# Mixing single accumulating transfers among the pair transfers of a segment sum, and six instead of twelve of them in front

## The chip, the cores and the metric

The kernel runs on one core of a Trainium2 chip. The metric is device time in microseconds (us), the median of several executions. The core's engines are TensorE (PE; PEld in the profile is its weight load), VectorE (DVE), ScalarE (ACT), GpSimd (POOL) and SyncE (SP, which here only issues transfers).

## What is computed

A layer of a graph network. There are N = 6250 nodes and 206250 edges, each with 128 features in float32; `row` is the source node of each edge.

```python
edge_aggr = jnp.zeros((n, HIDDEN), dtype=x.dtype).at[row].add(edge_features)
reps = n // global_feat.shape[0]
global_expand = jnp.repeat(global_feat, reps, axis=0)
combined = jnp.concatenate([x, edge_aggr, global_expand], axis=-1) @ W_c + b_c
h = jax.nn.softplus(combined @ W1 + b1)
h = jax.nn.softplus(h @ W2 + b2)
return h @ W3 + b3            # then: layernorm(x + this)
```

Nearly all of the time goes into the first line, the segment sum.

## The kernel before

**Two kinds of edges.** The edges are cut into columns, and every column takes one of two ways to the sum.

- *Pairs* (810 pairs of columns, 105 edges in a column). The edges are sorted into buckets of 256 nodes. ACT or DVE writes a one-hot matrix (`compare`, L869 and L876/L878), TensorE multiplies by it (`gather`, L887), ACT copies the result out of PSUM into one of six `pairs` buffers (`settle`, L898), and POOL sends each pair of columns with one indirect transfer to its place in a DRAM table `place` (L932). When a group of pairs is complete, SP reads `place` back as `chunks` (L579, issued through L176), DVE makes one-hots (`match`, L587), TensorE multiplies (`product`, L604), and DVE adds into `sums_t` (L617).
- *Own columns* (283, 128 edges in each). Edges of the same node are merged inside the column: TensorE spreads the node numbers (`name_own`, L810), DVE compares (`equal_own`, L819), TensorE sums (`sum_own`, L829), ACT copies (`ready_own`, L840), DVE writes the row numbers (`number_own`, L847/L849). POOL then adds the column to a copy of the totals in DRAM with one accumulating indirect transfer (L916). There are three copies, taken in turn; the first twelve own columns use copies 0 and 1 only, since copy 2 is zeroed later (`zero(2)`). An addition to a copy waits until the one before it on that copy has landed. The copies are read back and joined at the end.

**Groups and pieces.** There are nine groups, with (own, pairs) of (18, 20), (14, 80), (22, 130), four times (31, 130), (66, 40), (20, 20), and 19 own columns after the last pair. The two `place` tables alternate from group to group. Own columns and pairs are handled in pieces of up to three columns or three pairs. In each group the pieces are merged by their relative position, so that pieces of three own lie evenly among the pieces of three pairs; in group 0, LEAD = 12 own columns stand ahead of the first pair.

**The order of the work.** The order on TensorE, DVE, ACT and SP is the order in which the program emits the steps. It comes from planned times: the first transfer at FIRST = 13 us, then SCATTER = 1.3 us for every pair and ADDED = 1.87 us for every own column. Every piece's earlier steps are placed ahead of its planned time: its rows are loaded 34 us ahead, the gather 14 us, the settling copy 10.5 us, and so on. `over(...)` spreads other work over a span of the plan: the positions for the next group's pairs (`positions`, L343 to L556), the filling of the next table (`fill_rows`), and the reduction of the group before (`reduce_steps`, L558). All events are sorted by planned time and emitted. POOL's transfers are tied to the emitted order wherever an own column is next to another transfer.

The reduction of a group starts at the start of the next group. Its first chunk load on SP waits until all pair transfers of its group have landed, and whatever SP issues after it waits too.

The transfers of POOL share eight completion semaphores in turn. A settling copy reuses a `pairs` buffer six pieces later and waits for the three transfers out of it.

Of the kernel before, what the change touches and what calls it, by code (L numbers as in the profile page):

```python
# [13 lines left out]
ALU = mybir.AluOpType  # L14
# [36 lines left out]
COPIES = EACH  # L51
EARLY = (0, 1) * 6


SCATTER, ADDED = 1.3, 1.87
LOADED, CODED, COMPARED, GATHERED, SETTLED = 34.0, 21.0, 17.5, 14.0, 10.5
NAMED, EQUALLED, SUMMED, READY, NUMBERED = 20.0, 17.5, 14.0, 10.5, 7.5
FIRST = 13.0
LEAD = 12
SHARES = {0: 2, 1: 2, 2: 2}  # L60
SHARE = 3
PREP, SUM, FILLED = 0.85, 0.97, 0.6
# [7 lines left out]
BANKS = 3  # L70

TABLES = 6
NO_SYNC = mybir.DependencyInfo(mybir.DependencyClass.NoSync, mybir.DependencyReason.SCHED_ONLY)


@with_exitstack
def kernel(
# [23 lines left out]
    nc = tc.nc  # L101
# [67 lines left out]
    def copy_rows(k, a, b):  # L169
        return totals_at[k][a:b, :]  # L170
# [4 lines left out]
    def put_dma(engine, out, in_):  # L175
        ins = engine.dma_start(out, in_).ins  # L176
        if put["last"] is not None and put["tied"]:
            tc.add_manual_dep(ins, put["last"].name, NO_SYNC, reason="one order of all transfers")
        put["last"] = ins

    def rows_dma(out, in_):
        for _ in range(2):
# [2 lines left out]
        put_dma(nc.sync, out, in_)  # L185

    def sync_dma(out, in_):
        put_dma(nc.sync, out, in_)

    def node_rows_of(pool, n0, n, bufs=2):  # L190
        t = pool.tile([P, 4, D], F32, name="x_sb", bufs=bufs)
# [7 lines left out]
    with ExitStack() as phase:  # L199
# [358 lines left out]
        def reduce_steps(g):  # L558
# [16 lines left out]
            def load(i):  # L575
                b, lo, hi, _ = loads[i]
                t = chunks_p.tile([P, LOAD_CHUNKS, ROW], F32, name="chunks")
                chunks[i] = t
                sync_dma(t[:, :hi - lo].rearrange("p j c -> p (j c)"),  # L579
                         src_rows[(b * room + lo) * P:(b * room + hi) * P, :].rearrange(  # L580
                             "(p j) c -> p (j c)", p=P))

            def match(n):
                i, a, e = halves[n]
# [63 lines left out]
        def node_rows():  # L648
# [91 lines left out]
            steps.append(lambda: store(blocks_at[-1]))  # L740
            return steps

        pieces, ring, pair_no = [], {}, {}
        LATE = groups[-1][1]

        def own_pieces(g, a, b):
            own = [(g, "own", c, min(EACH, min(b, T) - c), P) for c in range(a, min(b, T), EACH)]
            if R and a < b == TC:
                own.append((g, "own", T, 1, R))
            return own  # L750

        for g, (a, b, _, _, s0, s1) in enumerate(groups):
            own = own_pieces(g, a, b)
            pairs = [(g, "pair", t, min(PAIRS, s1 - t), P) for t in range(s0, s1, PAIRS)]
            lead = 0 if g else LEAD // EACH
            mixed = sorted([((k + 0.5) / len(l), l[0][1], l[k]) for l in (own[lead:], pairs) if l
                            for k in range(len(l))])
            pieces += own[:lead] + [m[2] for m in mixed]
        last_pair = len(pieces) - 1
        pieces += own_pieces(G - 1, LATE, TC)  # L760
        for i, piece in enumerate(pieces):
            if piece[1] == "own":
                ring[i] = len(ring)
# [142 lines left out]
                nc.gpsimd.reg_mov(limits[rows], rows)  # L906
            return limits[rows]

        def scatter_rows(i):
            g, kind, c, k, r = pieces[i]  # L910
            if kind == "own":
                at, rows = own_of.pop(i)
                for j in range(k):
                    n = c + j
                    copy = EARLY[n] if n < len(EARLY) else n % COPIES
                    s = nc.gpsimd.indirect_dma_start(  # L916
                        out=copy_rows(copy, 0, N + 2),
                        out_offset=bass.IndirectOffsetOnAxis(ap=at[:r, j:j + 1], axis=0),
                        in_=rows[:r, j, :D], in_offset=None, bounds_check=limit(N + 1),
                        oob_is_err=False, compute_op=ALU.add)  # L920
                    if issued["last"] is not None:
                        tc.add_manual_dep(s.ins, issued["last"].name, NO_SYNC,
                                          reason="one order of all scatters")
                    issued["last"], issued["own"] = s.ins, True
                return
            rows_at.pop(i)
            rows = sets_at.pop(i)
            dst = places[place_of[g]][:rows_of[g], :].rearrange("(n two) c -> n (two c)", two=2)
            last = rows_of[g] // 2 - 1
            for j in range(k):  # L930
                at = pair_of[g][:, c - groups[g][4] + j:c - groups[g][4] + j + 1]
                s = nc.gpsimd.indirect_dma_start(  # L932
                    out=dst, out_offset=bass.IndirectOffsetOnAxis(ap=at, axis=0),
                    in_=rows[:, j].rearrange("p a b -> p (a b)"), in_offset=None,
                    bounds_check=limit(last), oob_is_err=False)
                if issued["own"]:
                    tc.add_manual_dep(s.ins, issued["last"].name, NO_SYNC,
                                      reason="one order of all scatters")
                issued["last"], issued["own"] = s.ins, False
                tc.declare_no_dep(s.ins, group="scatter",  # L940
                                  reason="no two edges of a group have one position")
                tc.add_to_no_dep_group("scatter", s.ins)

        bucket_at = {}

# [64 lines left out]
        with tc.manual_schedule(engines={ET.PE, ET.DVE, ET.Activation, ET.SP}):  # L1010
# [17 lines left out]
            tables()  # L1028
            nc.vector.memset(fill, -1.0)

            begins = []
            now = FIRST
            for _, kind, _, k, _ in pieces:
                begins.append(now)
                now += (SCATTER if kind == "pair" else ADDED) * k
            early = [i for i, t in enumerate(begins) if t < LOADED]

            def zero(k):
# [31 lines left out]
            def when(t, step):  # L1070
                events.append((t, len(events), step))
# [5 lines left out]
            for i, t in enumerate(begins):  # L1077
                if t >= LOADED:
                    when(t - LOADED, lambda i=i: load_rows(i))
                if pieces[i][1] == "own":  # L1080
                    when(t - NAMED, lambda i=i: name_own(i))
                    when(t - EQUALLED, lambda i=i: equal_own(i))
                    when(t - SUMMED, lambda i=i: sum_own(i))
                    when(t - READY, lambda i=i: ready_own(i))
                    when(t - NUMBERED, lambda i=i: number_own(i))
                else:
                    when(t - CODED, lambda i=i: code_rows(i))
                mine = units(i)
                for u, unit in enumerate(mine):
                    late_by = SCATTER * pieces[i][3] * u / len(mine)  # L1090
                    when(t - COMPARED + late_by, lambda unit=unit: compare(unit))
                    when(t - GATHERED + late_by, lambda unit=unit: gather(unit))
                    when(t - SETTLED + late_by, lambda unit=unit: settle(unit))
                when(t, lambda i=i: scatter_rows(i))
            over([more_tables, lambda: node_codes(0)] + positions(0), -8.0, FIRST + ADDED * LEAD - 19.0)
            over(fill_rows_0, -2.0, FIRST + ADDED * LEAD - 14.0)
            when(FIRST + ADDED * LEAD - 13.0, lambda: zero(2))
            when(4.0, rest_of_nodes)
            for g in range(1, G):
                a, b = groups[g][:2]  # L1100
# [16 lines left out]
            for g in range(G):  # L1117
                mine = [q for q in range(len(pieces)) if pieces[q][0] == g]
                t0 = begins[mine[0]]
                t1 = begins[mine[-1]] + (SCATTER if pieces[mine[-1]][1] == "pair" else  # L1120
                                         ADDED) * pieces[mine[-1]][3]
                prep = []
                for k in range(g + 1 + (g > SOONER), min(G, g + 2 + (g >= SOONER))):
                    prep += [lambda k=k: node_codes(k)] + positions(k)
                if NODES[0] <= g < NODES[1]:
                    upto = len(nodes)
                    if g + 1 < NODES[1]:
                        upto = 3 + (upto - 3) * (g + 1 - NODES[0]) // (NODES[1] - NODES[0]) // 4 * 4
                    part = nodes[held:upto]
                    held = upto  # L1130
                    middle = t0 + PREP * (t1 - t0)
                    over(part, middle, t1)
                    over(prep, t0, middle)
                else:
                    over(prep, max(t0, 34.0), t0 + PREP * (t1 - t0))
                if g == G - 1:
                    middle = max(t0 + 0.65 * (t1 - t0), begins[last_pair] + 9.0)
                    over(reduce_steps(g - 1), t0, middle)
                    over(reduce_steps(g), middle, t1 + 2.0)
                elif g:  # L1140
                    over(reduce_steps(g - 1), t0, t0 + SUM * (t1 - t0))
                over(fill_rows(g + 1), t0, t0 + FILLED * (t1 - t0))
# [284 lines left out]
```

## Time and profile before

| | |
|---|---|
| median of 3 runs | 1998.59 us (1998.35 to 2001.69) |
| profiled execution | 2005.1 us, its span 2002.9 us |
| mean granted clock of TensorE | 0.879 |
| PE busy | 1630.5 us (81%) |
| PEld busy | 1395.4 us (70%) |
| DVE busy | 1233.2 us (62%) |
| ACT busy | 1174.0 us (59%) |
| POOL busy | 1298.9 us (65%) |

Times of a group of instructions are written as busy time, mean of one in ns, idle time of the engine just ahead of them, and what ended most of that idle time. A window's line gives its length and then each engine's busy time in it. In a timeline, the number in brackets is how long the engine was idle before, and what released it; several instructions of one line are drawn together (x6). A busy TensorE can hold waits inside, since the ends of matmuls are modelled.

Group 0's transfers take 24 to 104 us of the span, groups 1 to 6 run from 104 to 1608 us, group 7 to 1788, group 8 to 1853, the 19 late own columns to 1888, and the joining of the copies and the dense layers to the end.

### The profile page before, as it was taken

What the parts mean: (1) busy time and instruction counts of PE and PEld (TensorE: products, weight loads), DVE (VectorE), ACT (ScalarE), POOL (GpSimd) and SP (SyncE); (2) the same over time, 40 slices, a digit from 0 to 9 for tenths busy, and PEclk for the clock granted to TensorE, in tenths of its full rate; (3) what the DMA queues carried; (4) which work ended last, traced back from release to release, by engine and by line L of the source; (5) the groups of instructions that cost most, each with busy time, mean ns of one, the idle gap of its engine ahead of it and who ended that gap; (6) DMA issues with size and microseconds to landing.
All of it is one profiled execution on the core that took longest, in us unless ns stands there. A gap on an engine that the chain in (4) does not pass through costs nothing. (4 is left out here: it accounts for less than half of the span.)

```text
span 2002.9 us, 30974 instructions
## 1 busy us (share of the span) xinstructions
PE 1630.5 (81%) x10093; PEld 1395.4 (70%) x10093; DVE 1233.2 (62%) x2726; ACT 1174.0 (59%) x2921; POOL 1298.9 (65%) x1163
## 2 busy tenths in 40 slices
PE   5567777886889897998898888887888899969585
PEld 4456666775778776887676777766777788868464
DVE  7556645665556664676665776754555467756537
ACT  4255565666766666776677575666776654333045
POOL 2666565666666666666666665557666678778845
PEclk9577677888899989898998898899999899989888
DMA  9686465866777676876767666669777599966872
GB/s 338 164 253 184 140 194 163 236 190 178 214 210 202 196 204 192 237 215 181 209 183 237 190 191 174 185 168 265 207 213 214 156 249 227 229 148 164 211 207 66
DMA packets 401839, 399.72 MB, mean 200 GB/s; under 512 B 34286, under 2 KB 331323, under 8 KB 401673
## 3 DMA queue, kind: packets, MB, share of 16 engines
q1 hardware_dynamic: 322073, 275.77, 47.7%
q0 software_dynamic: 79600, 121.90, 23.5%
q8 instruction: 84, 1.38, 0.3%
q14 instruction: 82, 0.67, 0.1%
HBM read 245.79 MB, written 161.24 MB: 203 GB/s over the span
## 5 line engine op out<-in xcount | busy, mean ns | idle before, releaser
L932 POOL DMA_INDIRECT place<-pairs,pair x810 | 796.3, 983 | 420.9 <-issue 210.1
L604 PE MATMUL part<-hot,chunks 128*128 128x256 f32 x3440 | 928.8, 410 | 68.0 <-DVE hot L587 27.2
L898 ACT COPY pairs<-sorted 64x387 f32<-64x387 f32 (+2 forms) x1100 | 521.4, 474 | 588.3 <-PE sorted L887 213.1
L604 PEld LDWEIGHTS part<-hot,chunks 128*128 128x128 f32 x3440 | 663.2, 206 | 178.5 <-issue 59.7
L587 DVE SCALAR_TENSOR_TENSOR hot<-chunks,both_ps 128x512 f32<-128x512 f32 (+2 forms) x614 | 542.0, 896 | 221.8 <-PE part L604 105.4
L887 PE MATMUL sorted<-rows,sort_hot 105*128 105x129 f32 x3240 | 528.8, 307 | 90.0 <-ACT sort_hot L878 26.6
L887 PEld LDWEIGHTS sorted<-rows,sort_hot 105*128 105x128 f32 x3240 | 483.1, 216 | 156.4 <-issue 45.3
L916 POOL DMA_INDIRECT totals_at<-own_sum,own_at x283 | 440.4, 1556 | 227.7 <-issue 101.2
L876 ACT ACTIVATE sort_hot<-by_slot,slot 105x128 f32<-105x128 f32 x1006 | 331.7, 394 | 3.7
L878 ACT ACTIVATE sort_hot<-sort_hot,ones 105x384 f32<-105x384 f32 (+1 forms) x341 | 208.5, 611 | 11.1
L840 ACT COPY own_sum<-sorted 128x387 f32<-128x387 f32 (+3 forms) x99 | 46.3, 467 | 146.0 <-PE sorted L829 92.9
L869 DVE TENSOR_TENSOR sort_hot<-slot,both_ps 105x384 f32<-105x384 f32 (+1 forms) x209 | 112.5, 539 | 2.7 <-PE sorted L887 2.0
L819 DVE TENSOR_TENSOR same<-sorted,src_i 128x384 f32<-128x384 f32 (+3 forms) x99 | 53.0, 535 | 92.6 <-PE sorted L810 32.5
L423 DVE TENSOR_REDUCE slot<-small 105x20 f32<-105x500 f32 x81 | 54.8, 676 | 87.5 <-remote 29.4
L529 DVE TENSOR_SCALAR pair<-small,half_p 64x10 int32<-64x10 f32 x162 | 36.6, 226 | 114.2 <-remote 53.2
L829 PE MATMUL sorted<-own_rows,same 128*128 128x129 f32 x566 | 94.6, 303 | 9.1 <-issue 7.0
L829 PEld LDWEIGHTS sorted<-own_rows,same 128*128 128x128 f32 x566 | 85.1, 211 | 24.1 <-issue 17.9
L522 PEld LDWEIGHTS <-spread 104*128 104x128 bf16 x810 | 30.9, 100 | 69.7 <-DVE spread L511 39.7
L522 PE MATMUL small<-jump,spread 104*128 104x4 bf16 x810 | 33.7, 166 | 53.7 <-DVE spread L511 31.8
L617 DVE TENSOR_TENSOR sums_t<-sums_t,part 128x512 f32<-128x512 f32 (+1 forms) x104 | 68.3, 660 | 6.8 <-PE part L604 4.9
L417 PEld LDWEIGHTS <-ones_h 104*105 104x105 bf16 x405 | 37.5, 147 | 47.4 <-issue 40.8
L511 DVE TENSOR_TENSOR spread<-both_ps,starts 104x640 bf16<-104x640 f32 x81 | 66.8, 824 | 1.7
(179 smaller groups left out, 1081.6 us busy)
## 6 DMA issues: line engine op xcount, KB each, us to landing
rows<-in_edge_attr SPq DMA_DIRECT2D x266, 315.0 KB
chunks<-place SPq DMA_DIRECT2D x125, 408.0 KB
chunks<-place SPq DMA_DIRECT2D x120, 340.0 KB
own_rows<-in_edge_attr SPq DMA_DIRECT2D x91, 192.0 KB
chunks<-place SPq DMA_DIRECT2D x49, 272.0 KB
place<-pairs,pair POOLq DMA_INDIRECT x810
totals_at<-sums_t SPq DMA_DIRECT2D x3, 3072.0 KB
late<-totals_at SPq DMA_DIRECT2D x36, 256.0 KB
```

Of the source, the lines that this page charges most:

```text
L511: nc.vector.tensor_tensor(past, twice_ps[:KB].unsqueeze(1).to_broadcast([KB, per_set, P]), own["starts"][:, q0:q0 + per_set].unsqueeze(2). ...
L587: nc.vector.scalar_tensor_tensor(hot[:, :e - a], chunks[i][:, a:e, D:W].to_broadcast([P, e - a, BL]), code_of(g), iota_ps.unsqueeze(1).to_ ...
L604: nc.tensor.matmul(part[:, b % 2, :], t[:, q, :D], hot[:, q - a], start=(lo + q == 0), stop=(last and q == hi - lo - 1))
L617: nc.vector.tensor_add(here, here, new)
L829: nc.tensor.matmul(out[:r, j, :], same[:r, j, :r], rows_at[i][:r, j, :], start=True, stop=True)
L869: nc.vector.tensor_tensor(hot[:PN, :m], slot[:PN, at:at + 2 * m - 1:2].unsqueeze(2).to_broadcast([PN, m, P]), slot_ps[:PN].unsqueeze(1).to ...
L876: nc.scalar.activation(hot[:PN, j], by_slot[:PN], AF.Abs, bias=slot[:PN, at:at + 1], scale=-1.0)
L878: nc.scalar.activation(hot[:PN, :m], hot[:PN, :m], AF.Relu, bias=ones[:PN, :1], scale=-1.0)
L887: nc.tensor.matmul(out[:, j, :], hot[:PN, j], rows_at[i][:PN, 2 * (lo + j) + n, :], start=True, stop=True)
L898: nc.scalar.copy(sets_at[i][64 * n:64 * n + 64, lo:lo + m, h, :W], out[64 * h:64 * h + 64, :m, :])
L916: s = nc.gpsimd.indirect_dma_start(out=copy_rows(copy, 0, N + 2), out_offset=bass.IndirectOffsetOnAxis(ap=at[:r, j:j + 1], axis=0), in_=ro ...
L932: s = nc.gpsimd.indirect_dma_start(out=dst, out_offset=bass.IndirectOffsetOnAxis(ap=at, axis=0), in_=rows[:, j].rearrange("p a b -> p (a b ...
```

## The change

Two things change in the order of POOL's transfers.

1. Own columns and pairs of a group are no longer merged by pieces of three but singly: a list `issues` holds (piece, index in the piece), and `scatter_row(i, j)` issues one transfer where `scatter_rows(i)` issued a piece's three. In groups 3 to 6 this puts one own column after every four or five pairs, in groups 1 and 2 after every five or six. A piece's planned time is that of its first transfer.
2. LEAD becomes 6. The end of the spans for `positions(0)` and `fill_rows(0)` hangs on LEAD and moves from 16.4 to 5.2 us and from 21.4 to 10.2 us of the plan; `zero(2)` stays at 22.2 (22.4 before).

Besides, the first chunk load of each group is given explicit dependencies on the last twelve pair transfers of its group.

```diff
-LEAD = 12
+LEAD = 6
+LANES = 12
+SYNC = mybir.DependencyInfo(mybir.DependencyClass.Sync, mybir.DependencyReason.DATA)
...
-                sync_dma(t[:, :hi - lo].rearrange("p j c -> p (j c)"),
+                ins = sync_dma(t[:, :hi - lo].rearrange("p j c -> p (j c)"),
...
+                if i == 0:
+                    for late in lasts[g][-LANES:]:
+                        tc.add_manual_dep(ins, late.name, SYNC, reason="every row is there")
...
             lead = 0 if g else LEAD // EACH
-            mixed = sorted([((k + 0.5) / len(l), l[0][1], l[k]) for l in (own[lead:], pairs) if l
-                            for k in range(len(l))])
-            pieces += own[:lead] + [m[2] for m in mixed]
+            parts = [(p, j) for p in own[lead:] for j in range(p[3])]
+            both = [(p, j) for p in pairs for j in range(p[3])]
+            mixed = [(p, j) for p in own[:lead] for j in range(p[3])] + [
+                m[2] for m in sorted([((k + 0.5) / len(l), l[0][0][1], l[k])
+                                      for l in (parts, both) if l for k in range(len(l))],
+                                     key=lambda m: m[:2])]
+            for p, j in mixed:
+                if not j:
+                    pieces.append(p)
+                issues.append((p, j))
...
-            begins = []
+            begins, ends, at_time = [None] * len(pieces), [None] * len(pieces), []
             now = FIRST
-            for _, kind, _, k, _ in pieces:
-                begins.append(now)
-                now += (SCATTER if kind == "pair" else ADDED) * k
+            for p, j in issues:
+                i = number[p]
+                if not j:
+                    begins[i] = now
+                at_time.append((now, i, j))
+                now += SCATTER if p[1] == "pair" else ADDED
+                ends[i] = now
...
-                when(t, lambda i=i: scatter_rows(i))
+            for t, i, j in at_time:
+                when(t, lambda i=i, j=j: scatter_row(i, j))
             over([more_tables, lambda: node_codes(0)] + positions(0), -8.0, FIRST + ADDED * LEAD - 19.0)
             over(fill_rows_0, -2.0, FIRST + ADDED * LEAD - 14.0)
-            when(FIRST + ADDED * LEAD - 13.0, lambda: zero(2))
+            when(FIRST + ADDED * LEAD - 2.0, lambda: zero(2))
```

`scatter_row(i, j)` holds the same two transfers as `scatter_rows(i)` at L916 and L932, without the loops over `j`, and keeps a list `lasts` of each group's pair transfers.

More of the change, by code (lines that the diff above doesn't have):

```diff
@@ L179, in put_dma @@
         put["last"] = ins
+        return ins
     def rows_dma(out, in_):
@@ L187, in sync_dma @@
     def sync_dma(out, in_):
-        put_dma(nc.sync, out, in_)
+        return put_dma(nc.sync, out, in_)
     def node_rows_of(pool, n0, n, bufs=2):
@@ L741, in node_rows @@
             return steps
+        lasts = {}
         pieces, ring, pair_no = [], {}, {}
         LATE = groups[-1][1]
+        issues = []
         def own_pieces(g, a, b):
@@ L755 @@
             lead = 0 if g else LEAD // EACH
-            mixed = sorted([((k + 0.5) / len(l), l[0][1], l[k]) for l in (own[lead:], pairs) if l
-                            for k in range(len(l))])
-            pieces += own[:lead] + [m[2] for m in mixed]
+            parts = [(p, j) for p in own[lead:] for j in range(p[3])]
[8 more added lines that the diff above has]
+                issues.append((p, j))
         last_pair = len(pieces) - 1
-        pieces += own_pieces(G - 1, LATE, TC)
+        for p in own_pieces(G - 1, LATE, TC):
+            pieces.append(p)
+            issues += [(p, j) for j in range(p[3])]
+        number = {p: i for i, p in enumerate(pieces)}
         for i, piece in enumerate(pieces):
@@ L907, in limit, with scatter_row @@
             return limits[rows]
-        def scatter_rows(i):
+        def scatter_row(i, j):
             g, kind, c, k, r = pieces[i]
             if kind == "own":
[L912 to L936, printed above, removed]
@@ new lines, in scatter_row @@
+                at, rows = own_of[i]
+                n = c + j
+                copy = EARLY[n] if n < len(EARLY) else n % COPIES
+                s = nc.gpsimd.indirect_dma_start(
+                    out=copy_rows(copy, 0, N + 2),
+                    out_offset=bass.IndirectOffsetOnAxis(ap=at[:r, j:j + 1], axis=0),
+                    in_=rows[:r, j, :D], in_offset=None, bounds_check=limit(N + 1),
+                    oob_is_err=False, compute_op=ALU.add)
+                if issued["last"] is not None:
@@ L937, in scatter_rows @@
                     tc.add_manual_dep(s.ins, issued["last"].name, NO_SYNC,
                                       reason="one order of all scatters")
[L939 to L942, printed above, removed]
+                issued["last"], issued["own"] = s.ins, True
+                return
@@ new lines, in scatter_row @@
+            rows = sets_at[i]
+            dst = places[place_of[g]][:rows_of[g], :].rearrange("(n two) c -> n (two c)", two=2)
+            at = pair_of[g][:, c - groups[g][4] + j:c - groups[g][4] + j + 1]
+            s = nc.gpsimd.indirect_dma_start(
+                out=dst, out_offset=bass.IndirectOffsetOnAxis(ap=at, axis=0),
+                in_=rows[:, j].rearrange("p a b -> p (a b)"), in_offset=None,
+                bounds_check=limit(rows_of[g] // 2 - 1), oob_is_err=False)
+            if issued["own"]:
+                tc.add_manual_dep(s.ins, issued["last"].name, NO_SYNC,
+                                  reason="one order of all scatters")
@@ L944 @@
+            issued["last"], issued["own"] = s.ins, False
+            tc.declare_no_dep(s.ins, group="scatter",
+                              reason="no two edges of a group have one position")
+            tc.add_to_no_dep_group("scatter", s.ins)
+            lasts.setdefault(g, []).append(s.ins)
         bucket_at = {}
@@ L1119 @@
                 t0 = begins[mine[0]]
-                t1 = begins[mine[-1]] + (SCATTER if pieces[mine[-1]][1] == "pair" else
-                                         ADDED) * pieces[mine[-1]][3]
+                t1 = max(ends[q] for q in mine)
                 prep = []
```

## The prediction

> **What bounds the kernel now.** I read the windows of busy time first, one per group of edges, then the waits, then the timeline at single stalls of POOL, then the times at which TensorE's semaphore moved.
>
> The page gives POOL two jobs: 810 pair transfers and 283 own (accumulating) transfers.
>
> ```profile
> L932 POOL DMA_INDIRECT place<-pairs,pair x810 | 796.3, 983 | 420.9 <-issue 210.1
> L916 POOL DMA_INDIRECT totals_at<-own_sum,own_at x283 | 440.4, 1556 | 227.7 <-issue 101.2
> ```
>
> Where nothing waits, the timeline has 1.28 us from one pair to the next and 1.87 us from one own to the next (0.3 us of each is POOL's step between instructions). So a group needs pairs x 1.28 + own x 1.87. The windows (the columns after the length are PE, PEld, DVE, ACT, POOL, then the clock) show a middle group and the group with many own columns:
>
> ```profile
> 525.00:793.00 268.00, 232.25 (x1492) 198.83 (x1491) 173.46 (x352) 183.17 (x463) 176.04 (x161) 0.92 0.74 209
> 1611.00:1788.00 177.00, 160.89 (x976) 144.03 (x976) 118.59 (x210) 74.31 (x187) 142.57 (x107) 0.96 0.85 213
> ```
>
> Group 3 needs 31 x 1.87 + 130 x 1.28 = 224 us and takes 268; group 7 needs 66 x 1.87 + 40 x 1.28 = 175 and takes 177. Summing POOL's idle time beyond 0.3 us by group gives 41.7 (group 0, 21.1 of it before the first transfer), 40, 42, 45, 44, 62, 33, then 5 and 2. So POOL sets the pace at the tail; groups 1 to 6 (104 to 1608 us) hold 267 us in which POOL waits for data. TensorE is no full explanation: 87% busy in group 3, 91% in group 7.
>
> What makes it wait shows at a stall of POOL (1448.29 to 1451.25). ACT's settling copies, TensorE and POOL:
>
> ```profile
> 1441.31 0.97 ACT L898 COPY pairs<-sorted 64x387 f32<-64x387 f32 x2 [1.35 <-PE part L604]
> 1445.67 0.97 ACT L898 COPY pairs<-sorted 64x387 f32<-64x387 f32 x2 [3.16 <-PE sorted L829]
> 1450.01 0.97 ACT L898 COPY pairs<-sorted 64x387 f32<-64x387 f32 x2 [3.36 <-remote]
> ```
> ```profile
> 1442.63 0.83 PE L887 MATMUL sorted<-rows,sort_hot 105*128 105x129 f32 x6
> 1445.26 2.32 PE L604 MATMUL part<-hot,chunks 128*128 128x256 f32 x10
> 1450.80 1.42 PE L887 MATMUL sorted<-rows,sort_hot 105*128 105x129 f32 x5 [3.21 <-DVE sort_hot L869]
> ```
> ```profile
> 1447.31 0.98 POOL L932 DMA_INDIRECT place<-pairs,pair  x1 [0.30 <-issue]
> 1451.25 0.97 POOL L932 DMA_INDIRECT place<-pairs,pair  x1 [2.96 <-ACT rows L792]
> ```
>
> The copy at 1450.01 needs the gather recorded at 1442.63 to 1443.46, and ACT had been free from 1446.64. TensorE's semaphore moved for that gather only at 1449.99, 6.5 us after its recorded end; four later moves follow within 0.28 us, all after POOL had run dry at 1448.29. I matched the 1385 recorded moves of that semaphore, in order, with the recorded ends of the matmuls that make them. Median lateness 0.17 us, but it depends on what POOL is doing. In groups 2 to 6, by pairs issued since the last own transfer (mean lateness; share over 1.2 us): own in progress 0.41, 12%; 1st pair 0.15, 6%; 2nd 0.41, 14%; 3rd 1.68, 46%; 4th 2.72, 70%; 5th 4.29, 86%; 6th to 8th 3.2, 73%; 9th to 12th 1.6, 41% (by then POOL has often stalled). By stretch the share over 1.2 us is 0 in 24 to 67 us (only own transfers), 29 to 47% in groups 1 to 6, and 2% in group 7, where no run of pairs exceeds three. The waits say the same: in 525 to 1608 us, then in 1611 to 1788 us (sum, times, longest):
>
> ```profile
> DVE hot L587 <- PE part L604: 76.6, 35, 6.3
> ```
> ```profile
> DVE hot L587 <- PE part L604: 17.2, 29, 1.3
> ```
>
> So long runs of pair transfers make TensorE's signals late; ACT, DVE, SP and then TensorE stand still, and POOL runs dry. Own transfers or idle time on POOL clear it.
>
> **The change, part by part. Single mixing, groups 1 to 6.** Runs of 12 to 16 pairs with three own between become runs of 4 or 5 pairs (130 to 31) or 6 (130 to 22, 80 to 14) with one own between. Weighting the shares above by POOL's time, a cycle in groups 3 to 6 of 3 own and 12 pairs has 40% late; of 1 own and 4.2 pairs, 30%. With 5.8 pairs it is 41%, no better than now. Lateness also ends sooner, since the next own is at most two pairs away (2.6 us), not eight. The full gain has a bound: TensorE's work taken to group 7's clock and share (232.25 x 0.92/0.96 / 0.91 = 245 in group 3) or POOL's need, whichever is longer, saves 23, 24, 31 and 30 in groups 3 to 6 and 42 and 40 in groups 2 and 1: 190 us. Against: those shares come from runs that began after three own transfers (5.6 us); a single one may clear less. In 67 to 104 us, where POOL alternates 6 pairs, 2 own, 4 pairs, 1 own, 4 pairs, 3 own, 47% were late, and 0.8 us into the four pairs behind the single own a signal was 3.9 us late. So the term lies between -190 and +39 (the second below). I take 30% of the 184 us of idle in groups 3 to 6, since their share over 1.2 us falls by a quarter and the longest delays go, and nothing for groups 1 and 2: **-55**.
>
> By the Trainium skill (SBUF — State Buffer, "Who interferes with whom") PE and ACT never wait on anyone, and transfers do not contend with compute engines; then the order on POOL could not move TensorE's signals, and this term would be nought. The trace speaks against reading it so here: 2% late beside 41%.
>
> **More changes between own and pair.** The first pair after an own has a pitch of 1.32, the second 1.30: 0.06 us per change. There were 82, there will be 233. In groups 1 to 6 (103 more, 6.2 us) POOL's idle time covers it; if that cover goes, it costs the 6. In groups 0, 7 and 8 (48 more) POOL has no slack: **+3**. The same copy of the totals is added to every third own, in group 7 every 3 x 1.87 + 1.8 x 1.28 = 7.9 us instead of 5.6; 7.4 us each was needed in the crowded head, so nothing is lost.
>
> **Six own in front.** The head is now:
>
> ```profile
> 24.00 1.77 POOL L916 DMA_INDIRECT totals_at<-own_sum,own_at  x1 [21.40 <-ACT own_sum L840]
> 65.33 1.55 POOL L916 DMA_INDIRECT totals_at<-own_sum,own_at  x1 [1.87 <-DMA rows<-in_edge_attr]
> 67.19 1.02 POOL L932 DMA_INDIRECT place<-pairs,pair  x1 [0.31 <-ACT rows L792]
> ```
>
> Twelve own in 43.2 us, 3.6 each, mostly waiting for the copy's previous addition; the group ends at 103.9. With six the first pair comes 21.6 us after the start, and 20 pairs and 12 own follow in 48 us plus 1 us of changes. From 24.0 that ends at 94.6 if nothing waits. But the positions of group 0 now stand on DVE ahead of the first own numbers (written at 22.7 to 23.1); they finish at 32.2 now, so the first own moves to 24 to 32, and the end to 95 to 103, plus stalls in the pairs (the same stretch has none over 0.3 us now). The group's loads start only when its last transfer lands. I take an end at 102: **-2**, ends -8 and +3.
>
> **Ends of groups.** SP's first chunk load waits for the last transfers (1.4 us after the last pair at 103.9), with row loads queued behind it on SP, for which TensorE's gathers wait later. An own now stands two pairs before that end; bounds 0 and, by a lane held for one more own and one pair, +3 per group, +24 in all. I take **0**: the load names pairs alone, and the load queue runs 34 us ahead in the plan. The twelve added dependencies are waits that those lanes already served.
>
> **Sum.** -55 +3 -2 = -54 from the profiled execution's 2005.1 gives 1951. That run lies 6.5 above the median of the runs shown (1998.59), so the prediction for the median is **1944**, its own case between 1905 and 1985.
>
> **Rivals.**
> *All of it clears* (0.16): one own every four pairs drains the delay fully, as in group 7. For: 2% late there. Against: group 7 has 1.65 own per pair, here one to four. It gives up to -190; halfway to it -120, 1875 to 1880.
> *Slower* (0.28): a single own of 1.87 us does not clear, so the clean stretches after three own (9 of every 24 us) go and every run is late. For: the 3.9 us above. Price: the idle of groups 1 to 6 grows with the share late, 267 x (47/41 - 1) = +39, which gives 2038; it decides as soon as over about 41% of signals are late. Against: singles at 512 and 785 us were followed by two or three clean pairs.
> *Nothing* (0.12): the late signals come from something other than POOL's order, or TensorE's 87% is the bound and lateness only chooses where POOL waits. Then only +3 -2 is left, to within some 4 us: 1999 or 2000. The rule of the Trainium skill above (SBUF — State Buffer) would be this case.
> The likeliest has 0.44.
>
> **How the numbers follow.** A measurement of this kernel can tell about 0.2%, 4 us, from no change. Faster takes the first two cases and a sixth of *nothing*: 0.62; same half of *nothing*: 0.06; slower 0.32. The range from 1870 to 2030 leaves out half of the full gain (0.08) and some 0.1 of the slower case, whose upper part has the ends of groups in it.
>
> **What would show it.** Right: POOL's idle in groups 3 to 6 falls from 33-62 to some 20-45 each, DVE's longest wait for L604 falls from 6.3 us to 4 or less, the share of late signals to about 30%, the clock there rises above 0.92, the first pair stands at 46 to 54 us. Wrong: signals late already at the first pair after a single own, or POOL's idle unchanged while lateness falls (TensorE bound), or SP's waits for place growing beyond 1.4 us per group.

## The result and the profile after

| | before | changed |
|---|---|---|
| median | 1998.47 us | 1950.29 us (1942.05 to 1954.14, 4 runs) |
| ratio | | 0.9763 (95% interval 0.9732 to 0.9795) |
| profiled execution | 2005.1 us, span 2002.9 | 1942.05 us, span 1940.2 |
| mean granted clock | 0.879 | 0.902 |

The change is worth 48 us in the median and 63 us between the two profiled executions. POOL's two lines in the page of the changed kernel (L946 and L933 are L932 and L916 of before):

```profile
L946 POOL DMA_INDIRECT place<-pairs,pair x810 | 803.9, 992 | 408.1 <-issue 216.8
L933 POOL DMA_INDIRECT totals_at<-own_sum,own_at x283 | 441.3, 1560 | 172.6 <-issue 75.7
```

They are 8 us busier, and the idle time ahead of them is 68 us less. The windows of groups 3 and 7 of the changed kernel (length, PE, PEld, DVE, ACT, POOL, clock):

```profile
507.60:770.10 262.50, 228.73 (x1484) 195.69 (x1484) 173.29 (x350) 184.02 (x468) 177.35 (x162) 0.94 0.76 214
1552.30:1728.40 176.10, 159.92 (x976) 143.70 (x976) 115.92 (x209) 74.04 (x185) 142.83 (x106) 0.96 0.86 208
```

Group 3 went from 268 to 262 us with TensorE's clock at 0.94 instead of 0.92; group 7 is as it was. From group start to group start the 62.7 us of span are: group 0 nothing, groups 1 to 6 9.9, 8.2, 4.9, 7.9, 21.3 and 6.5, from group 7 to the last transfer 0.7, the end of the kernel 3.3.

The head of the changed kernel, on POOL:

```profile
32.30 1.78 POOL L933 DMA_INDIRECT totals_at<-own_sum,own_at  x1 [29.70 <-DMA place<-fill]
51.18 1.55 POOL L933 DMA_INDIRECT totals_at<-own_sum,own_at  x1 [0.53 <-DMA totals_at<-sums_t]
53.03 1.03 POOL L946 DMA_INDIRECT place<-pairs,pair  x1 [0.30 <-issue]
```

The first own is 8.3 us later, the first pair 14.2 us earlier, and the group ends at 103.9 us in both kernels.

DVE's wait for a hot buffer in groups 3 to 6 of the changed kernel, and in group 7 (sum, times, longest):

```profile
DVE hot L593 <- PE part L610: 34.8, 26, 3.7
```
```profile
DVE hot L593 <- PE part L610: 15.5, 22, 1.3
```

Its longest fell from 6.3 to 3.7 us. The view puts a wait down to the matmul that ended last before it; the waits of the same line that it puts down to the gathers still reach 4.8 us in groups 3 to 6 (6.2 before):

```profile
DVE hot L593 <- PE sorted L905: 38.1, 22, 4.8
```

And the semaphore of TensorE is not on time more often. Some of its moves are missing from the trace, so each recorded move was paired, in order, with the latest end of a matmul that it can belong to. In groups 1 to 6, 49% of the moves are over 1.2 us late (40% before), the mean is 1.95 us (1.61). A count without any pairing says the same: 37% of the moves there stand within 0.1 us behind the recorded end of a matmul, and 50% did before.

What changed is the place of the late signals. By pairs since the last own, in groups 2 to 6, the mean lateness is now 2.3 (own in progress), 2.0, 1.8, 2.0, 2.1, 1.8, 1.8: flat, where it ran from 0.15 up to 4.3 and back. In groups 0, 7 and 8, with no more than two pairs in a row, no signal is over 1.2 us late.

It is the signals that are late, not the matmuls. At the stall of the kernel before that the prediction shows, the five moves from 1449.99 to 1450.27 us belong, by this pairing, to matmuls recorded to end from 1443.46 to 1447.58 us. Between the first and the last of these ends lie 4 us of recorded work, between the moves 0.29 us.

Where the 59 us of groups 1 to 6 (1503 to 1444 us) went can be read from TensorE alone. Its idle time there fell by 10 us (253 to 243; gaps over 2 us from 41 with 127 us to 30 with 102). Its busy time fell by 50 (1251 to 1201) for the same matmuls. The granted clock stood at half for 356 us before and for 259 after: 97 us at half speed are 48 us of work. This is an account of one engine's time; it does not show that the clock is the cause (in `paced_mid` below, groups 1 to 6 take 54 us less again, with 254 us at half clock). One such spell in the kernel before, a stall and what follows it (length, PE, PEld, DVE, ACT, POOL, clock):

```profile
1448.00:1451.00 3.00, 0.20 (x1) 0.23 (x2) 2.48 (x4) 0.96 (x2) 0.29 (x1) 0.90 0.59 165
1451.00:1458.00 7.00, 7.00 (x25) 6.17 (x26) 4.64 (x11) 6.83 (x20) 5.53 (x5) 0.56 0.97 278
```

TensorE stands still for 3 us, and for the 7 us after it works at 0.56: on TensorE, this stall is paid for twice. By the Trainium skill (TensorE: Matmul & The Clock Gate, Part 1) half rate is the default, which about 3.4 us of idleness brings back and about 3.4 us of activity lifts. The trace agrees in the unit: the spells last whole multiples of 3.4 us. It does not bear out the length of the idleness. Behind this gap of 1.75 us, half clock was granted from 1426.5 us on, for 3.4 us:

```profile
1426.40 2.86 PE L604 MATMUL part<-hot,chunks 128*128 128x256 f32 x6 [1.75 <-DVE hot L587]
```

### The profile page after: what moved, and what is told of

Same layout as the page of the kernel before. It is cut to its first block, busy times and chain, and to the rows that moved or that the text cites. A ratio compares the mean times of both kernels' runs of the same rounds, so it can differ in the third digit from the quotient of the medians.

```text
span 1940.2 us, 31028 instructions
## 1 busy us (share of the span) xinstructions
PE 1583.2 (82%) x10093; PEld 1361.1 (70%) x10093; DVE 1232.8 (64%) x2726; ACT 1170.5 (60%) x2921; POOL 1307.0 (67%) x1163
## 4 chain that ended last, share of the span: by engine, by line
PE 43%; ACT 6%; issue 5%; DVE 5%; DMA 3%; POOL 3%; another core or an unknown queue 1%; SPq 1%; ACTq 0%; DVEq 0%; POOLq 0%
PE part L610 25%; PE sorted L905 9%; ACT pairs L916 3%; PE sorted L847 2%; POOL place L946 2%; ACT sort_hot L894 2%; DMA place<-pairs,pair 1%; PE late_ps L1315 1%; PE sorted L828 1%; DVE hot L593 1%; POOL totals_at L933 1%; DMA x_sb<-in_x 1%; SPq L178 1%; ACT sort_hot L896 1%
## 5 line engine op out<-in xcount | busy, mean ns | idle before, releaser
L946 POOL DMA_INDIRECT place<-pairs,pair x810 | 803.9, 992 | 408.1 <-issue 216.8
L610 PE MATMUL part<-hot,chunks 128*128 128x256 f32 x3440 | 899.0, 401 | 59.3 <-DVE hot L593 24.2
L916 ACT COPY pairs<-sorted 64x387 f32<-64x387 f32 (+2 forms) x1100 | 521.0, 474 | 518.4 <-PE sorted L905 155.9
L610 PEld LDWEIGHTS part<-hot,chunks 128*128 128x128 f32 x3440 | 644.8, 200 | 156.2 <-issue 33.9
L593 DVE SCALAR_TENSOR_TENSOR hot<-chunks,both_ps 128x512 f32<-128x512 f32 (+2 forms) x614 | 541.3, 896 | 176.2 <-PE part L610 56.7
L905 PE MATMUL sorted<-rows,sort_hot 105*128 105x129 f32 x3240 | 510.7, 300 | 78.6 <-issue 31.2
L905 PEld LDWEIGHTS sorted<-rows,sort_hot 105*128 105x128 f32 x3240 | 466.4, 209 | 145.4 <-issue 61.7
L933 POOL DMA_INDIRECT totals_at<-own_sum,own_at x283 | 441.3, 1560 | 172.6 <-issue 75.7
```

The source lines that it names most:

```text
L593: nc.vector.scalar_tensor_tensor(hot[:, :e - a], chunks[i][:, a:e, D:W].to_broadcast([P, e - a, BL]), code_of(g), iota_ps.unsqueeze(1).to_ ...
L610: nc.tensor.matmul(part[:, b % 2, :], t[:, q, :D], hot[:, q - a], start=(lo + q == 0), stop=(last and q == hi - lo - 1))
L905: nc.tensor.matmul(out[:, j, :], hot[:PN, j], rows_at[i][:PN, 2 * (lo + j) + n, :], start=True, stop=True)
L916: nc.scalar.copy(sets_at[i][64 * n:64 * n + 64, lo:lo + m, h, :W], out[64 * h:64 * h + 64, :m, :])
L933: s = nc.gpsimd.indirect_dma_start(out=copy_rows(copy, 0, N + 2), out_offset=bass.IndirectOffsetOnAxis(ap=at[:r, j:j + 1], axis=0), in_=ro ...
L946: s = nc.gpsimd.indirect_dma_start(out=dst, out_offset=bass.IndirectOffsetOnAxis(ap=at, axis=0), in_=rows[:, j].rearrange("p a b -> p (a b ...
```

## The experiments

Ratios are to the kernel before, run beside it on the same chip. The columns after it are for groups 1 to 6, in us: length, POOL's stalls (its gaps over 0.9 us between two transfers, less the usual 0.3), share of TensorE's signals over 1.2 us late (paired as above), time at half clock.

| kernel | ratio (interval) | length | stalls | late | half clock |
|---|---|---|---|---|---|
| before | | 1503 | 264 | 40% | 356 |
| changed | 0.9763 (0.9732 to 0.9795) | 1444 | 191 | 49% | 259 |
| changed_again | 0.9872 (0.9815 to 0.9930) | 1481 | 229 | 49% | 314 |
| lead_only | 0.9974 (0.9935 to 1.0013) | 1508 | 270 | 39% | 379 |
| mix_only | 0.9770 (0.9708 to 0.9831) | 1437 | 187 | 48% | 260 |
| matches_ahead | 0.9779 (0.9727 to 0.9831) | 1448 | 198 | 48% | 272 |
| paced_pairs | 0.9901 (0.9870 to 0.9932) | 1472 | 217 | 48% | 311 |
| paced_mid | 0.9454 (0.9416 to 0.9493) | 1390 | 6 | 20% | 254 |
| paced_blocks | 0.9927 (0.9891 to 0.9963) | 1493 | 165 | 39% | 309 |
| paced_best | 0.9462 (0.9412 to 0.9513) | 1413 | 69 | 65% | 199 |

**Each half of the change alone.** The first run has `LEAD = 6` in the kernel before, with `zero(2)` at the same planned time; the second has `LEAD = 12` in the changed one.

> Only the six own columns in front; pieces of three stay together. In the changed kernel the first own transfer starts at 32.3 instead of 24.0 us and group 0 still ends at 103.9 us as before, so theory T (the gain comes from mixing singly, which spreads POOL's load evenly) expects 1990 to 2003 us, no gain beyond 0.2%. Rival H (the head's rearrangement, with positions earlier on DVE, is what pays, and the later groups inherit it) expects 1960 to 1980.

> Single mixing with twelve own columns in front. T expects the changed kernel's time within 0.3%, 1945 to 1957 us, group 0 ending at 100 to 107 us and the idle time of POOL in groups 1 to 6 near 200 us. H expects 1970 to 1990.

Six in front alone: 0.9974, not told from no change. Its head has the changed kernel's times:

```profile
31.78 1.78 POOL L916 DMA_INDIRECT totals_at<-own_sum,own_at  x1 [29.18 <-DMA rows<-in_edge_attr]
52.31 1.03 POOL L932 DMA_INDIRECT place<-pairs,pair  x1 [0.30 <-issue]
```

Its group 0 ends at 100.9 us, and groups 1 to 6 take 1508 us. Single mixing with twelve in front gives 0.9770, all of the gain; its group 0 ends at 104.9. Theory T held (1943.82 us is 1 us below its range), H fell. `mix_only` keeps the explicit dependencies of the first chunk loads; no run took them out, so that they have no part in the gain is not shown.

**More room for DVE.** Five `hot` buffers instead of four, `TOGETHER = 3`.

> The changed kernel with five hot buffers instead of four and three matches ahead of the products instead of two. If late signals cost time through DVE, which waits for TensorE to free a hot buffer (176 us of idle time at that line in the changed kernel), the time falls by 10 to 30 us. If they cost it through the settling copies alone, it stays within 0.3% of 1950.

1949.56 us, the changed kernel's time. But the added buffer did not take DVE's wait away. The changed kernel, then this one:

```profile
L593 DVE SCALAR_TENSOR_TENSOR hot<-chunks,both_ps 128x512 f32<-128x512 f32 (+2 forms) x614 | 541.3, 896 | 176.2 <-PE part L610 56.7
```
```profile
L593 DVE SCALAR_TENSOR_TENSOR hot<-chunks,both_ps 128x512 f32<-128x512 f32 (+2 forms) x614 | 541.5, 895 | 177.9 <-PE part L610 60.5
```

The idle time ahead of that line is 177.9 us instead of 176.2, so the run does not tell whether this wait costs time.

**Pacing the pairs.** Behind each pair transfer of the changed kernel:

```diff
+            pad = nc.gpsimd.memset(idle_p, 0.0)      # [128, PAD]
+            tc.add_manual_dep(pad.ins, s.ins.name, NO_SYNC, reason="behind its transfer")
+            issued["last"], issued["own"] = pad.ins, True
```

PAD = 32:

> The changed kernel with one small memset on POOL behind every pair transfer, so that two pairs in a row have a pitch of about 1.5 to 1.6 us instead of 1.28. POOL's need in groups 3 to 6 grows from 224 to about 255 to 265 us. Theory L (POOL's pair rate is what makes TensorE's signals late) expects the share of signals over 1.2 us late in groups 1 to 6 to fall from 49% to under 15%, POOL's idle time there from 200 to under 60 us, and the time within 1% of the changed kernel's, 1930 to 1970. The rival (the late signals have another cause, for example the load of the hardware queues) expects the share to stay at 40 to 50% and the time to grow by 50 us or more, since part of the memsets adds to the stalls.

This did not pace them. On POOL:

```profile
905.47 0.99 POOL L948 DMA_INDIRECT place<-pairs,pair  x1 [0.16 <-issue]
906.44 0.17 POOL L960 MEMSET idle_p<- 128x32 f32 x1
906.77 0.97 POOL L948 DMA_INDIRECT place<-pairs,pair  x1 [0.17 <-issue]
```

The memset fits into the 0.3 us between two transfers, the pitch is 1.30 us, and the late share stays at 48%. The time is 0.9901 of the kernel before, more than the changed kernel's 0.9763 and little more than the 0.9872 of its second result; whether these memsets cost anything is not shown.

PAD = 512, and three kernels that leave work out:

> The changed kernel with a memset of 512 elements a partition on POOL behind every pair transfer; the memset of 32 elements took 0.15 us and vanished in the 0.3 us between two instructions (pitch 1.30), so that run did not pace the pairs. This one should give a pitch of 1.5 to 1.9 us and a POOL need of 255 to 300 us in groups 3 to 6 (262, 261, 267, 249 us long in the changed kernel). Theory L (pair transfers issued at 1.28 us make TensorE's signals late) expects the share over 1.2 us in groups 3 to 6 to fall from 44-60% to under 20% and POOL to be busy nearly throughout, so groups as long as POOL's need. Rival R (late signals come from elsewhere) expects the share to stay over 40% and each group to be longer than POOL's need by 20 us or more.

> The changed kernel without the 283 accumulating transfers; all other work on own columns stays, and their sums do not reach the output. POOL's need in groups 3 to 6 is 166 us instead of 224. L expects runs of pairs with no break: share over 1.2 us at 50% or more, half-clock time of TensorE in groups 1 to 6 above 267 us, groups 3 to 6 at 245 to 265 us each, although POOL has 58 us less to do. R, or a bound by POOL's need, expects these groups to shrink by 10 us or more each.

> The changed kernel without the 810 pair transfers; both place tables are zeroed by SP at the start (some 38 MB, which delays the head by 100 to 250 us and is read out by looking at groups 3 to 6 alone). The rest of the work stays; the pairs' sums are left out of the output. L expects under 5% of signals over 1.2 us late, hardly any time at half clock, and groups 3 to 6 at 225 to 245 us each (TensorE's busy time at full clock). R expects 30% or more late and groups within 10 us of the changed kernel's 249 to 267.

> The changed kernel with half of each pair transfer: 128 rows of 136 elements instead of 272, to positions half as far into the zeroed table, so as many rows and half the bytes; the other half of the sorted rows is left out. Under L, if the bytes in flight make the signals late, the share over 1.2 us in groups 3 to 6 falls to 25% or less and the groups shrink by 10 us or more; if the number of rows does, the share stays at 40 to 60% and the groups within 6 us of the changed kernel's.

They took 2066.34, 1607.89, 1687.79 and 1815.20 us. But the kernel before took 1734.00 us beside them, on another chip than the one of the runs above, where it took 1995 us. So these four don't decide between L and R, because no signal was late there: in each of the four, 99.9% of TensorE's recorded moves stand within 0.1 us behind the recorded end of a matmul. What they do show, one execution each, is the kernel without late signals. Group 3 of `half_rows`, with the full number of transfers at the usual pitch:

```profile
521.40:747.30 225.90, 209.72 (x1492) 188.77 (x1492) 172.45 (x349) 183.35 (x465) 176.83 (x161) 0.95 0.79 208
```

It takes 225.6 us where POOL needs 224.4, with less than 1 us of idle time on POOL beyond the usual 0.3. The kernel before was not traced on this chip, but its 1734.00 us fit as well: POOL's need of groups 1 to 6 (1234 us) and the rest of its trace above (104 us ahead of them, 395 behind) make 1733, an estimate. And with the own or the pair transfers left out, TensorE is the bound, at full clock, over 500 us of each:

```profile
500.00:1000.00 500.00, 493.04 (x3626) 444.52 (x3625) 423.12 (x888) 428.45 (x1086) 297.00 (x306) 1.00 0.86 250
```
```profile
500.00:1000.00 500.00, 494.38 (x3575) 445.64 (x3574) 414.92 (x854) 431.09 (x1093) 114.81 (x74) 1.00 0.75 185
```

At 3626 matmuls in 500 us, the 1486 of a middle group would take 205 us: an estimate of TensorE's own bound, 19 us below POOL's need.

**The changed kernel again, and a middling pace.** The second run has PAD = 256.

> The changed kernel as it is, beside the kernel before. Two kinds of chip have shown up: on one the kernel before takes about 1995 us and TensorE's signals come late; on another it took 1734 us, the kernel with halved rows ran groups 1 to 6 at POOL's need with no idle time, and no signal was late. Theory K (the change gains only where signals are late, by making the stalls shorter; elsewhere POOL sets the pace and the extra changes between own and pair cost 0.06 us each) expects 0.972 to 0.982 of the kernel before on the first kind, and on the second 0.2 to 0.8% slower than it, 1737 to 1748 us. The rival (single mixing is worth it by itself, through fewer waits on the same copy or a better order of the other engines) expects 1 to 2.5% faster on either kind.

> The changed kernel with a memset of 256 elements behind each pair transfer: pitch about 1.47 us, POOL's need 251 us in groups 3 to 6. On a chip with late signals theory L (the rate of pair transfers makes them late) expects the share over 1.2 us in groups 3 to 6 to fall from 44-60% to under 25%, half-clock time in groups 1 to 6 from 267 to under 200 us, and the time to be between 1930 and 1970 us; the rival (lateness independent of POOL's rate) expects the share to stay over 40% and the time at 1990 us or more. On a chip without late signals POOL's need alone counts: 0.19 us more for each of 810 pairs, 150 us on top of the changed kernel's time.

The signals were late on this chip (49% in `changed_again`), and the changed kernel gave 0.9872: less than theory K's 0.972 to 0.982, and inside the rival's 1 to 2.5%. Its interval (0.9815 to 0.9930) lies below 1, but apart from the first result's (0.9732 to 0.9795): the change is a gain both times, of a size that does not repeat. What would part K and the rival, the chip without late signals, was not run.

The paced run says more. The pitch is 1.47 us:

```profile
907.08 0.97 POOL L948 DMA_INDIRECT place<-pairs,pair  x1 [0.17 <-issue]
908.05 0.33 POOL L960 MEMSET idle_p<- 128x256 f32 x1
908.55 0.98 POOL L948 DMA_INDIRECT place<-pairs,pair  x1 [0.16 <-issue]
```

and group 3 of `paced_mid` takes 251.5 us, about its need at that pitch, with no stall over 1 us in groups 2 to 6:

```profile
492.20:744.10 251.90, 216.34 (x1492) 189.66 (x1492) 174.79 (x349) 183.57 (x465) 220.49 (x291) 0.94 0.80 220
```

Late signals fall from 49% to 20%, none over 4.7 us, and the time to 1902.12 us: POOL does 810 memsets more, and the kernel is 4% faster than `changed_again` beside it. In groups 3 to 6, 13% are late, as L had it (under 25%). Two of L's other marks were missed: the time is below its 1930 to 1970 us, and the time at half clock is 254 us, not under 200. The rival's marks (over 40%, 1990 us or more) were missed by far. A memset alone does not do it, since those of 32 elements left the pitch and the share as they were. So on such a chip pair transfers at a pitch of 1.28 us make TensorE's signals late, and at 1.47 far fewer of them.

**Pacing with both orders.** PAD = 192 in groups 1 to 6 only (`if 0 < g < 7`), in the order of before and in the changed one.

> The kernel before (pieces of three own together, twelve own in front) with a memset of 192 elements behind each pair transfer of groups 1 to 6, pitch about 1.42 us, POOL's need 243 us in groups 3 to 6. If the pair rate alone makes the signals late, the order matters little once the pairs are paced: late share in groups 3 to 6 under 25%, time within 1% of the same pacing on the changed order. If own transfers spread singly are needed as well (runs of 12 pairs still build up lateness at a pitch of 1.42), the late share stays above that of the changed order by 15 points or more and the time is 1 to 3% longer. On a chip without late signals both cost about 90 us over the kernel before.

> The changed kernel with the same pacing, groups 1 to 6 only, pitch about 1.42 us. On a chip with late signals: 0.19 us less for each of 80 pairs and 0.05 less for 730 against the run with 256 elements (1902 us), so 1850 to 1885 us if signals stay as much on time (under 25% late), about 1890 to 1930 if the share goes back above 35%. This would beat both kernels.

At this pitch the order decides: 0.9927 in blocks (the order of before, three own together), 0.9462 singly, both beside the same runs of the kernel before. Group 3 of each, blocks first:

```profile
515.30:791.60 276.30, 231.65 (x1482) 201.12 (x1481) 172.99 (x349) 181.71 (x461) 211.43 (x291) 0.91 0.74 202
```
```profile
504.40:754.50 250.10, 223.12 (x1482) 193.19 (x1483) 174.59 (x348) 182.55 (x465) 213.57 (x291) 0.95 0.82 224
```

In blocks at a pitch of 1.42 us the delay sets in later in a run: 12% late at the 3rd pair, 36%, 51%, 66%, 83% at the 4th to 7th, where at 1.28 us it was 46% at the 3rd and 66% at the 4th. A delay that grows with every pair by the excess of some service time S over the pitch would pass 50% at 3.2 pairs in the one and at 5 in the other: 3.2 (S - 1.28) = 5 (S - 1.42) gives S near 1.67 us, an estimate. Runs of 12 still reach a mean of 4.5 us. Singly at the same pitch more signals are late (65% against 39%), but only 5% by over 5 us (11% in blocks), and POOL's stalls are 69 us instead of 165, the time at half clock 199 instead of 309. That the long delays are what costs is read from these counts.

Neither branch of the first expectation came: in groups 3 to 6 the paced blocks are late less often than the paced singles (40% against 70%), not more, and they take 4.9% longer, not 1 to 3%. Of the second, the branch for a share above 35% held: 1906.16 us lies in its 1890 to 1930. `paced_best` does beat both kernels, by as much as `paced_mid`.

The share does not simply follow the pitch, either. Singly it is 49% at 1.28 us, 65% at 1.42 and 20% at 1.47 (this one on another chip of the late kind than the 1.42). At 1.28 us POOL's own stalls interrupt the stream for some 200 us; that this is what keeps the share down there is not shown.

## Why the prediction was right, and where its steps were not

- **The total.** -54 us was forecast from the profiled execution, -63 came; the median is 1950 against 1944, and `mix_only` shows that the term I gave nearly all of it to, single mixing, carries it. Run again, the change was worth only 29 us in the median (`changed_again`), so the forecast's size is good to a factor of two and no better.
- **Single mixing: the size held, the mechanism failed.** I took 30% of the idle time of groups 3 to 6 because the late share would fall from 40 to 30%. It rose: from 42 to 52% in those groups. A single own transfer of 1.87 us does not clear the delay; that is the rival's condition, and it was met. The first sign of being wrong came too: 48% are late already at the first pair after a single own. That -55 fits all the same is luck. So is it that signs of being right came without the step behind them: POOL's idle of 24 to 42 us in each of groups 3 to 6, a clock of 0.94 to 0.95 there. (The stretch from 67 to 104 us, which I read against the term, has five pairs, not four, between its two and its one own; nothing hangs on it.) The rival's price failed too, since it let the idle time follow the share of late signals (+39 us). POOL's idle in groups 3 to 6 fell by 27%, from 184 to 135 us, all the same, and groups 1 and 2, for which I had taken nothing, gave 18 of the 59 us. What the runs put in place of the share is how the lateness is spread: the same or more of it, evenly, instead of a clean stretch followed by eight late pairs; fewer long gaps on TensorE, and 97 us less at half clock. The clock was not a term of my sum, and in TensorE's account of its time it makes up 48 of the 59 us. That the even spread makes the gaps rarer is read from those counts; no run changed the spread alone with the same share.
- **All of it clears.** Not singly at 1.28 us. At a pitch of 1.47 POOL's stalls are gone, though 20% of the signals are still late.
- **Own-to-pair changes.** 233, as counted. Of the +3, groups 7 and 8 had 39 changes more, 2.3 us. From the first transfer of group 7 to the last of all, POOL without its waits took 273.0 us before and 273.6 after: 0.6. In group 7 every pair now stands alone, so only the first pair's 0.04 us is paid. With the waits, which fell from 3.9 to 2.6 us, the stretch went from 277.0 to 276.3.
- **Six in front.** First own 32.3 (forecast 24 to 32), first pair 53.0 (46 to 54), end of the group 103.9 against 102: -2 was 0. The first own numbers are written at 31.0 us, right behind the last positions, and that ate the gain, a little beyond the upper bound (103). In blocks the -2 did come: the group ends at 100.9 in `lead_only`.
- **Ends of groups.** Taken at 0: the first chunk load follows the last transfer by 1.6, 1.7 and 3.3 us in the first three groups (1.4, 1.5 and 4.2 before). Right.
- **The rule on ports.** By the Trainium skill (SBUF — State Buffer, "Who interferes with whom") PE never waits on anyone. `paced_mid` measures against it a dependence of TensorE's signals on POOL's rate (49% and 20% late), though not that a port of SBUF is the place.

Open: what the pair transfers and TensorE's signals share, and why one chip does not have it. On the chips with late signals the traces also lack records, those of ACT and DVE too, whose signals are on time, and each execution on record has a granted clock from the profiler; so whether the recording has a part in the delay is not shown. On the chip without late signals POOL sets the pace, and the changed order should cost about 9 us there (151 changes x 0.06, an estimate); it was not run there. That halved rows on a chip with late signals would help was not tried either.

## What to carry to other kernels

POOL's stream of pair transfers did not show here as a busy engine: it showed as other engines released late, and a longer pitch (1.47 us instead of 1.28) shortened the kernel. Before a bound is read from busy shares, hold the times at which an engine's semaphore moves against the ends of its instructions. When TensorE's time is added up, look for half clock behind each of its gaps, as behind the 3 us above. And when a forecast comes true, hold its steps against the trace as well: here the late share moved the other way.

## What was not expected of the hardware

- The same kernel before took 1734 us on one chip and 1995 to 2014 us on two others. In the four kernels traced on the first, TensorE's signals were on time, and 1641 or more of some 1653 semaphore moves stand in the trace; on the others 1243 to 1462. There ACT's and DVE's moves are missing as well (in the kernel before 557 of 1550 and 799 of 2470).
- On such chips TensorE's semaphore moves up to 8 us and more after the recorded end of its matmul while POOL issues pair transfers at 1.28 us; those of ACT and DVE that are recorded follow their instructions within 0.02 us (99 of 100).
- 810 memsets of 0.35 us on POOL made the kernel 4% faster on such a chip.
